# New order of the first loads, a bias row spread by TensorE, warming products first, and re-written due times in a four-layer graph kernel

## The chip, the cores and the metric

The kernel runs on one core of a Trainium2 chip. The metric is the device time of one execution in microseconds (us), taken as the median of the runs. A core has five engines that work side by side, each through its own queue and in the order of that queue: TensorE (PE in the profile; PEld is its weight load), VectorE (DVE), ScalarE (ACT), GpSimd (POOL) and SyncE (SP, which only issues DMAs). They wait for each other through semaphores.

## The reference, cut to what matters

`x` has 128 matrices of 128 x 512 in float32, `adj` is 128 x 128, the weights are 512 x 512. Four layers follow each other, each with a residual and a layer norm over the last axis:

```python
# layer 0
y = einsum('nm,bmd->bnd', adj, x)
x = layernorm(x + y @ weight + bias)
# layer 1: attention without softmax; rel is masked with adj.T and divided by its row norm
rel = adj.T * ((x @ Wq.T) @ (x @ Wk.T).T); rel = rel / norm(rel, axis=2)
x = layernorm(x + rel @ (x @ Wv.T))
# layer 2: graph attention, masked with adj
h = x @ W;  e = leaky_relu(h@a1 [:, None] + h@a2 [None, :]) * adj
x = layernorm(x + elu(softmax(e) @ h + beta * h))
# layer 3: pre[b, o, d, n] = A[b, o, n] + C[b, o, d] - A[b, o, d], A = adj @ x, C = A + b
x = layernorm(x + max(relu(pre), axis=-1))
```

## The kernel before, in words

The 128 matrices are taken in 32 groups (NG) of four (G). A group's rows lie on the 128 partitions. Each large product by a 512 x 512 matrix is a Strassen-Winograd product: seven products of half-size blocks instead of eight, with sums of blocks ahead of them. `left_factors` (line 360) makes the sums of the left side on GpSimd (s1, s2, s3, s4; its four due times stand for s1, s2, s3, s4 in that order of the list), `weight_blocks` (line 157) those of the weights on VectorE, once for the whole kernel. `product` (line 535) makes the seven products, numbered 1 to 7, on TensorE in PSUM banks ("regions": 1, 6, 7 and 4 in bank r0; 5 and 3 in r12; 2 in a bank of tag pi). What belongs to one region is added up in place, so each `out` that reads it on VectorE or ScalarE must be done before the next product adds to it. From the second group on, products 2 and 4 are themselves Strassen products (`inner_product`, the pi rows of the profile). A group's layers are: `aggregate` (p_y), the y product by w0 (r_y), `stats` and `norm`; then `turn` or `turn_blocks` with `move` (x transposed by TensorE for groups 0 and 1, by VectorE and DMAs for the others), the m product (r_m, by Wq.T Wk, which is made once as m_qk by the qk product, r_qk), `scores` (p_rel), the v product (r_v), `attend` (p_o); then `gather` (p_z), the z product (r_z), exponential and elu; then `widen` (p_a), the maximum and the last norm.

The order of all this is written out by hand. `emit(at, f)` puts a piece of code on a list with a due time, and at the end the list is sorted by due time and run (line 1243). Pieces with equal due times keep the order in which they were put on the list. The engines are wrapped by `InOrder`, so each engine's queue has its instructions in exactly that order. Due times are only an order; 28 of their units are one group. `TABLE` (line 250) has the due times of every group, `FIRST` those of groups 0 and 1 where they differ, `LAST` those of the last three, and `STEPS` (line 445) the offsets within a product with inner products. Groups overlap: while one is in layer 3, others are in layers 2, 1 and 0.

At the start, adj, x[0], x[1], the bias (read by a DMA that repeats one row of 2 KB onto 128 partitions, 256 KB), x[2] and x[3] are loaded on SP's queue, w0 on ACT's queue (lines 93 to 125), then wq, wk, wv, w2 and small things on SP's. TensorE makes two products of the identity into banks r0 and r12 (lines 132 to 135), transposes adj, and makes eight products of the identity (`WARM`, lines 144 to 146). [...]for the y product the bias is put into the bank by a copy of ScalarE (`fill` in `product`, the row ACT r_y<-bias_sb) and the products then add to it. The fill of a region precedes its first product by `lead` in due time, for group 0 by 4.4.

All lines of the profile that say L26 are instructions made through `InOrder`; they are told apart by the names of their tiles.

Of the kernel before, what the change touches and what calls it, by code (L numbers as in the profile page):

```python
# [29 lines left out]
def kernel(  # L30
# [32 lines left out]
    nc = tc.nc  # L63
# [27 lines left out]


    adj_sb = const.tile([P, P], FP)
    nc.sync.dma_start(adj_sb, adj)
    x1, x2, x3 = {}, {}, {}

    def load(g):
        x1[g] = data.tile([P, G, D], FP, tag="x1", name=f"x1_{g}", bufs=3)
        if g == 0:
            for b in range(G):  # L100
                nc.sync.dma_start(x1[g][:, b, :], x[b])
                if b == 1:
                    nc.sync.dma_start(bias_sb, on_all(bias0, D))
        else:
            sync.dma_start(x1[g], x[g * G : (g + 1) * G].rearrange("b n d -> n b d"))

    bias_sb = const.tile([P, D], FP)
    load(0)
    w0_sb = const.tile([P, K, D], FP)
    nc.scalar.dma_start(w0_sb, w0.rearrange("(k p) f -> p k f", p=P))  # L110
    wq_sb = work.tile([P, K, D], FP, tag="tv", name="wq_sb")
    nc.sync.dma_start(wq_sb, wq.rearrange("(k p) f -> p k f", p=P))
    wk_sb = work.tile([P, K, D], FP, tag="c", name="wk_sb")
    nc.sync.dma_start(wk_sb, wk.rearrange("(k p) f -> p k f", p=P))
    wv_sb = work.tile([P, K, D], FP, tag="xB", name="wv_sb")
    nc.sync.dma_start(wv_sb, wv.rearrange("(k p) f -> p k f", p=P))

    w2_sb = const.tile([P, K, D], FP)
    nc.sync.dma_start(w2_sb, w2.rearrange("(k p) f -> p k f", p=P))
    a_sb = data.tile([P, 2, D], FP, tag="x3", name="a_sb", bufs=1)  # L120
    nc.sync.dma_start(a_sb.rearrange("p s d -> p (s d)"), on_all(a2, 2 * D))
    beta_sb = const.tile([P, 1], FP)
    nc.sync.dma_start(beta_sb, on_all(beta, 1))
    b3_sb = const.tile([P, 1], FP)
    nc.sync.dma_start(b3_sb, b3.rearrange("(p o) -> p o", o=1))
# [5 lines left out]

    for tag, n in (("r0", 1), ("r12", 1)):
        for i in range(n):
            r = psum.tile([P, 2, H], FP, tag=tag, name=f"first_{tag}_{i}", bufs=n)
            pe.matmul(r, ident, ident[:, None, :].to_broadcast([P, G, P]), start=True, stop=True)
    mhalf = const.tile([P, G], FP)
    dve.memset(mhalf, -0.5)

    adjT = const.tile([P, P], FP)
# [3 lines left out]

    warm = bank("p_warm")
    for i in range(WARM):
        pe.matmul(warm[:, :P], ident, ident, start=True, stop=True)
# [99 lines left out]
    def row(at, step, n=G):  # L246
# [4 lines left out]
        load=[-21.1232], y=[0.9608, 1.8251, 2.1487, 2.7922],  # L251
        y_sums=[4.5561, 5.0639, 6.7629, 6.9969], y_inner=[5.2833, 7.5035, 7.9599, 7.7423],
        y_w=[6.4865, 10.1067, 9.7011, 18.5098, 16.5578, 25.5346, 18.8593],
        stats0=[13.0727, 13.9676, 15.6348, 14.8804], norm0=[15.6928],
        apply0=[16.441, 16.56, 17.1055, 18.4252], turn=[16.9531, 18.9169, 15.0983, 23.7872],
        turn_blocks=[17.6387, 18.378, 19.3199, 18.8892], move=[21.2268, 20.1475, 23.7935, 24.4105],
        x_sums=[25.5484, 25.8887, 25.5714, 27.1546], x_inner=[27.0248, 27.3651, 27.6181, 27.4647],
        m=[28.2059, 29.9451, 30.7559, 39.3743, 35.0579, 32.0807, 31.5941],
        scores=[35.5574, 36.2751, 36.3095, 39.6263], masked=[40.1785], squares=[41.2658],
        turn_rel=[40.8158], move_rel=[43.2987, 45.3105, 45.5881, 44.1661], inverse=[42.7358],  # L260
        v=[41.1537, 34.8028, 35.2269, 32.9135, 36.819, 44.1908, 45.5822],
        attend=[51.1788, 52.5818, 53.9439, 54.1297], residual=[51.7575, 52.9793, 54.8472, 55.5115],
        squares1=[52.1071, 55.1681, 55.5885, 56.295], dots=[52.6394, 54.6161, 55.8601, 56.5298],
        norm1=[56.6185], scale=[58.0637], apply1=[67.3359, 67.3118, 68.311, 67.3949],
        spread=[61.4852], leaky=[62.1614], weighted=[62.3481], greatest=[63.6868], exps=[63.9389],
        divide=[64.6743], turn_att=[66.48], with_beta=[55.7842], turn_blocks_2=[65.0697],
        move_2=[65.6032], gather=[70.1205, 71.0446, 73.2368, 74.4083],
        z_sums=[74.7466, 74.9675, 75.3471, 79.5091], z_inner=[76.2873, 76.452, 76.7576, 79.7843],
        z_w=[76.5238, 78.3454, 80.9549, 82.1806, 80.3108, 74.0925, 83.986],
        exp=[84.1886, 85.0555, 95.1779, 97.9857], elu=[86.5931, 86.915, 97.0853, 99.5009],  # L270
        norm2=[100.4793], apply2=[101.1271, 102.2, 101.6434, 101.6261],
        widen=[102.9021, 104.404, 104.6097, 106.3071],
        top=[104.9696, 105.5877, 105.8825, 107.7194], norm3=[108.5946],
        apply3=[109.0064, 110.4459, 109.9895, 111.6524], store=[116.2428],
# [4 lines left out]
            y=[-0.9173, 0.2561, 2.5559, 2.6098], y_sums=[5.7842, 6.1923, 7.6412, 8.0217],  # L279
            y_w=[6.656, 6.9826, 8.5177, 10.5158, 10.5177, 12.1185, 12.1169],  # L280
            stats0=[14.8567, 15.0593, 15.0036, 15.7551], norm0=[16.1054],
            m=[26.9197, 27.6264, 27.6652, 28.2251, 29.8853, 32.0185, 32.0172],
            scores=[35.9958, 37.3155, 38.45, 39.3155], masked=[39.5575], squares=[42.4727],
            turn_rel=[41.0869], move_rel=[42.4032, 42.1994, 41.3572, 41.7949],
            v=[42.7111, 44.0451, 45.3088, 46.3784, 47.3081, 48.2976, 49.1509],
            attend=[50.3341, 51.6935, 52.7247, 53.3341],
            residual=[51.2419, 52.2419, 52.8787, 54.4537],
            squares1=[51.6342, 53.6777, 54.5661, 54.7798], norm1=[56.2059],
            apply0=[17.374, 17.6244, 18.5295, 18.0555], turn=[18.8709, 19.7935, 20.9961, 21.5866],
            dots=[55.2805, 58.6316, 60.212, 60.5925], scale=[61.2871], spread=[61.7827],  # L290
            leaky=[62.1], weighted=[62.205], greatest=[64.0362], exps=[64.0854], divide=[65.2555],
            turn_blocks_2=[65.6], move_2=[67.0921],
        ),
        1: dict(
            y=[-11.6669, -10.4156, -10.312, -9.8874], y_sums=[-3.77, -3.67, -1.551, 3.0174],
            y_w=[7.0161, 7.9774, 8.126, 9.7685, 10.9791, 11.4015, 12.7041],
            stats0=[14.0438, 14.1814, 14.7308, 15.7036], norm0=[17.4806],
            attend=[49.1976, 51.8422, 53.416, 53.4184],
            apply0=[18.4423, 19.1027, 20.4894, 18.5104], turn=[21.0277, 21.0846, 21.3846, 21.542],
            x_sums=[22.8224, 24.281, 27.507, 28.0022],  # L300
# [5 lines left out]
            exp=[0.4623, 11.611, 13.6093, 21.9374], elu=[6.6028, 13.5806, 17.1367, 22.1806],  # L306
            norm2=[23.3538], apply2=[25.0389, 27.3987, 25.9338, 25.563],
            squares3=[35.4179, 39.239, 38.0926, 41.5412],
            widen=[44.4948, 56.0663, 55.0979, 58.4343], top=[44.9981, 56.3795, 60.4284, 60.9337],
            norm3=[62.9017], apply3=[64.4412, 66.5207, 68.7228, 67.9152], store=[69],  # L310
        ),
        NG - 2: dict(
            scale=[4.3047], apply1=[4.6775, 11.0377, 10.4618, 10.2756], spread=[6.9011],
            leaky=[8.5406], weighted=[8.6149], greatest=[11.14], exps=[12.7308], divide=[14.9407],
            turn_att=[19.4796], with_beta=[20.9256], gather=[33.1448, 34.2964, 34.1197, 33.8382],
            z_sums=[37.1312, 37.1799, 37.2299, 38.9411],
            z_w=[37.2, 39.2089, 40.5339, 42.6626, 45.9385, 46.5626, 47.9032],
            exp=[51.1816, 51.9016, 53.9016, 58.1278], elu=[51.9326, 54.0745, 59.5933, 63.8365],
            norm2=[65.6683], apply2=[66.9349, 67.9136, 68.7218, 69.9541],
            widen=[72.5885, 69.738, 73.9565, 76.7205], top=[73.9072, 73.9667, 75.9682, 78.4954],  # L320
            stats3=[68.0781, 73.1502, 70.7817, 73.9103], norm3=[73.9726],
            apply3=[81.0356, 88.4294, 88.4341, 88.4354], store=[91.3384],
        ),
        NG - 1: dict(
            load_w2=[-23.6669], m=[-1.0223, 1.0487, 2.4676, 3.6749, 7.9692, 8.2221, 9.9221],
            scores=[10.4191, 11.0622, 12.0436, 13.2103], masked=[14.918], squares=[15.9336],
            turn_rel=[17.0025], inverse=[19.5602],
            v=[17.0016, 19.283, 20.9796, 22.8356, 24.6364, 26.4739, 27.9989],
            attend=[30.1034, 30.2339, 30.8373, 30.4857],
            residual=[30.4, 31.4552, 33.8743, 31.7856],  # L330
            stats1=[33.7623, 34.1537, 33.9623, 34.1488], norm1=[34.3934],
            dots=[34.3979, 35.5481, 35.1904, 40.2755], scale=[40.5527],
# [87 lines left out]
    def by_columns(p, a, b, first):  # L420

        for c in range(2):
            for k in range(2):
# [21 lines left out]
    STEPS = {  # L445
        "m": (
            {
                1: (-1.2981, -0.3541),
                6: (1.724, 2.1528),
                7: (3.0677, 3.3979),  # L450
                5: (4.5184, 5.1615),
# [822 lines left out]
```

## Time and profile before

| what | us |
|---|---|
| median of 3 runs | 2141.83 (2141.7 to 2141.99) |
| the profiled execution's own time | 2141.56 |
| its span, from the first to the last instruction | 2139.7 |
| TensorE busy | 2116.7 |
| VectorE busy | 1725.1 |
| ScalarE busy | 1293.5 |
| GpSimd busy | 954.3 |
| first aggregate product (p_y) starts | 7.38 |
| first product by a weight (r_y) starts | 11.73 |
| w0 landed | 6.54 |
| x[0], x[1], bias, x[2], x[3] landed | 6.89, 7.55, 9.10, 9.74, 10.42 |
| last product ends | 2128.2 |

Times in the profile are from the start of the span. A row of the timeline has its start, its length, the engine, the operation, its output and inputs by name with the sizes, how many instructions were merged into it (xN), and in brackets how long the engine had been idle before and for whom it waited. A product of float32 appears as two passes, so that one matmul of the kernel is two instructions in the profile. A row's length includes the time in which the last pass runs out; the next pass can start before that.

### The profile page before, as it was taken

To read this page: it belongs to the slowest core of one execution; us is meant where nothing else is said; L and a number is where in the kernel's file an instruction comes from. 1 tells how busy PE (TensorE), PEld (TensorE's weight loads), DVE (VectorE), ACT (ScalarE), POOL (GpSimd) and SP (SyncE) were. 2 spreads that over 40 slices of the span, in tenths; PEclk is the share of its full clock that TensorE was granted. 3 is DMA by queue.
4 is the path that set the end of the run, shared out by engine and by line. 5 is a ranking of instruction groups with operands and counts; after the bars stand their busy time and mean duration, and the time that the engine had idled before them with its cause. 6 is when DMAs were issued, how large, how long until landed. Compare 5 with 4: busy or idle time off the path is not lost.

```text
span 2139.7 us, 36859 instructions
## 1 busy us (share of the span) xinstructions
PE 2116.7 (99%) x12325; PEld 1836.7 (86%) x12325; DVE 1725.1 (81%) x4961; ACT 1293.5 (60%) x2950; POOL 954.3 (45%) x949
## 2 busy tenths in 40 slices
PE   9999999999999999999999999999999999999996
PEld 7888888888888888888888888888888898888883
DVE  5688887878888878878878888788888788888777
ACT  3336556666566666567665566665666665676655
POOL 4244455444455444454444554444554444544431
PEclk9999999999999999999999999999999999999998
DMA  4012232221232222323222322212322213332201
GB/s 174 25 36 54 66 75 69 57 73 51 73 76 70 55 60 60 78 72 75 55 54 66 76 69 57 73 52 72 75 70 55 60 60 77 72 74 55 54 27 59
DMA packets 362524, 139.66 MB, mean 65 GB/s; under 512 B 303200, under 2 KB 318688, under 8 KB 362336
## 3 DMA queue, kind: packets, MB, share of 16 engines
q1 hardware_dynamic: 361808, 136.27, 24.9%
q8 instruction: 98, 1.61, 0.3%
q10 hardware_dynamic: 528, 1.05, 0.2%
q14 instruction: 90, 0.74, 0.1%
HBM read 56.17 MB, written 41.48 MB: 46 GB/s over the span
## 4 chain that ended last, share of the span: by engine, by line
PE 94%; DVE 3%; SPq 1%; DMA 1%; POOL 0%; issue 0%; ACT 0%; ACTq 0%; DVEq 0%; POOLq 0%
PE r_m L26 13%; PE r_y L26 13%; PE r_v L26 12%; PE r_z L26 12%; PE p_rel L26 5%; PE p_y L26 5%; PE p_o L26 5%; PE p_z L26 5%; PE p_a L26 5%; PE pi_m L26 4%; PE pi_y L26 4%; PE pi_z L26 4%; PE pi_v L26 4%; SPq L26 1%; DVE x L26 1%; DVE st L26 1%
## 5 line engine op out<-in xcount | busy, mean ns | idle before, releaser
L26 ACT ACTIVATE x<-x,nmean,rstd 128x512 f32<-128x512 f32 x384 | 285.7, 805 | 180.9 <-DVE nmean L26 180.9
L26 ACT ACTIVATE scr<-x 128x512 f32<-128x512 f32 x360 | 226.2, 628 | 73.3 <-DVE x L26 69.0
L26 POOL TENSOR_TENSOR rstd<-ve,mhalf 128x4 f32<-128x4 f32 (+1 forms) x99 | 98.7, 997 | 294.9 <-DVE ve L26 294.8
L26 DVE SCALAR_TENSOR_TENSOR scr<-x,wa 128x512 f32<-128x512 f32 x256 | 174.8, 683 | 4.6
L26 POOL TENSOR_TENSOR rn<-n,mhalf 128x4 f32<-128x4 f32 x32 | 32.7, 1023 | 307.4 <-ACT sq L26 307.4
L26 DVE TENSOR_TENSOR x<-r_y,x 128x512 f32<-128x512 f32 x194 | 129.3, 679 | 31.7 <-PE r_y L26 27.6
L26 DVE TENSOR_TENSOR c<-pi_z,c 128x128 f32<-128x128 f32 x420 | 123.5, 306 | 26.9 <-ACT c L26 18.4
L26 DVE SCALAR_TENSOR_TENSOR x<-p_o,rn,x 128x512 f32<-128x512 f32 x128 | 95.4, 745 | 58.4 <-PE p_o L26 58.1
L26 DVE TENSOR_TENSOR tT<-pi_m,tT 128x128 f32<-128x128 f32 x420 | 121.8, 305 | 22.3 <-PE pi_m L26 16.1
L26 ACT COPY r_y<-bias_sb 128x512 f32<-128x512 f32 x64 | 38.0, 593 | 161.4 <-DVE tT L26 161.3
L26 PE MATMUL p_z<-eT,x 128*128 128x128 f32 x1024 | 135.1, 275 | 0.3 <-DVE x L26 0.3
L26 POOL TENSOR_TENSOR s_x<-xT 128x512 f32<-128x512 f32 x64 | 80.6, 1280 | 121.5 <-DMA xT<-xB 73.1
L26 PEld LDWEIGHTS p_z<-eT,x 128*128 128x128 f32 x1024 | 129.2, 192 | 5.4 <-DVE x L26 1.3
L26 PE MATMUL p_a<-x,adjT 128*128 128x512 f32 x256 | 128.8, 607 | 5.1 <-ACT x L26 4.3
L26 PE MATMUL p_y<-adjT,x 128*128 128x128 f32 x1024 | 129.9, 275 | 0.5 <-DMA x<-in_x_dram 0.5
L26 PE MATMUL p_rel<-xT,tT 128*128 128x128 f32 x1024 | 129.8, 275 | 0.0
L26 ACT COPY yT<-p_y 128x512 f32<-128x512 f32 x128 | 74.8, 584 | 88.2 <-PE p_y L26 88.2
L26 PEld LDWEIGHTS p_y<-adjT,x 128*128 128x128 f32 x1024 | 124.5, 192 | 2.4 <-issue 0.7
L26 PEld LDWEIGHTS p_rel<-xT,tT 128*128 128x128 f32 x1024 | 124.7, 192 | 1.8
L26 PE MATMUL p_o<-v,relT 128*128 128x512 f32 x256 | 125.7, 594 | 0.3 <-ACT xT L26 0.2
L26 DVE TENSOR_TENSOR x<-pi_y,x 128x128 f32<-128x128 f32 x420 | 118.9, 300 | 6.3
L26 PE MATMUL r_m<-s_x,t_m 128*128 128x256 f32 x512 | 123.7, 384 | 0.0
(244 smaller groups left out, 6067.5 us busy)
## 6 DMA issues: line engine op xcount, KB each, us to landing
out_dram<-x SPq DMA_DIRECT2D x128, 256.0 KB, 2.0
x<-in_x_dram SPq DMA_DIRECT2D x31, 1024.0 KB, 7.7
xT<-xB SPq DMA_DIRECT2D x480, 64.0 KB, 2.3
relT<-relB SPq DMA_DIRECT2D x496, 16.0 KB, 1.8
eBd<-eB SPq DMA_DIRECT2D x30, 256.0 KB, 2.0
eT<-eBd SPq DMA_DIRECT2D x120, 64.0 KB, 1.9
s<-s2d SPq DMA_DIRECT2D x29, 256.0 KB, 5.1
w_sb<-in_L_gnn_weight_dram ACTq DMA_DIRECT2D x1, 1024.0 KB, 5.8
```

Source lines behind the costliest of these rows:

```text
L26: return lambda *args, **kw: self.tc.keep_in_program_order(op(*args, **kw))
```

## The change

The loads are issued on SP's queue in this order: adj, the bias, x[0] to x[3], w0, wq, wk, wv, w2, the small ones. The bias comes as one row of 512 numbers onto one partition (`bias_row`, which shares its memory with x2). A row of ones beside it is the left factor of two products of one row, which write the bias on all 128 partitions into the banks r0 and r12; ScalarE copies r12 into `bias_sb`. These products take the place of the two products of the identity. The eight warming products go ahead of the transpose of adj. The fill's lead for group 0 becomes 0.7, as for the other groups (0.2 for group 1). The due times of all tables are new; the products' arithmetic and the number of the other instructions are as before.

```diff
     adj_sb = const.tile([P, P], FP)
-    nc.sync.dma_start(adj_sb, adj)
+    sync.dma_start(adj_sb, adj)
...
             for b in range(G):
-                nc.sync.dma_start(x1[g][:, b, :], x[b])
-                if b == 1:
-                    nc.sync.dma_start(bias_sb, on_all(bias0, D))
+                sync.dma_start(x1[g][:, b, :], x[b])
...
     bias_sb = const.tile([P, D], FP)
+    bias_row = data.tile([1, D + P], FP, tag="x2", name="bias_row")
+    sync.dma_start(bias_row[:, :D], on_one(bias0, D))
     load(0)
     w0_sb = const.tile([P, K, D], FP)
-    nc.scalar.dma_start(w0_sb, w0.rearrange("(k p) f -> p k f", p=P))
+    sync.dma_start(w0_sb, w0.rearrange("(k p) f -> p k f", p=P))
...
-    for tag, n in (("r0", 1), ("r12", 1)):
-        for i in range(n):
-            r = psum.tile([P, 2, H], FP, tag=tag, name=f"first_{tag}_{i}", bufs=n)
-            pe.matmul(r, ident, ident[:, None, :].to_broadcast([P, G, P]), start=True, stop=True)
     mhalf = const.tile([P, G], FP)
     dve.memset(mhalf, -0.5)
 
+
+    warm = bank("p_warm")
+    for i in range(WARM):
+        pe.matmul(warm[:, :P], ident, ident, start=True, stop=True)
     adjT = const.tile([P, P], FP)
     pt = bank("p_adjT")
     pe.transpose(pt[:, :P], adj_sb, ident)
     dve.tensor_copy(adjT, pt[:, :P])
-
-    warm = bank("p_warm")
-    for i in range(WARM):
-        pe.matmul(warm[:, :P], ident, ident, start=True, stop=True)
...
     FIRST = {
         0: dict(
-            y=[-0.9173, 0.2561, 2.5559, 2.6098], y_sums=[5.7842, 6.1923, 7.6412, 8.0217],
-            y_w=[6.656, 6.9826, 8.5177, 10.5158, 10.5177, 12.1185, 12.1169],
...
+            y=[-1.77, 2.4, 2.4, 2.4], y_sums=[2.52, 3.99, 5.05, 4.97],
+            y_w=[3.1, 8.75, 7.87, 10.61, 10.49, 12.11, 11.88], stats0=[13.25, 13.68, 13.75, 14.7],
...
-            apply0=[17.374, 17.6244, 18.5295, 18.0555], turn=[18.8709, 19.7935, 20.9961, 21.5866],
+            apply0=[18.13, 18.21, 18.36, 18.21], turn=[18.55, 19.1, 19, 18.61],
...
         "m": (
             {
-                1: (-1.2981, -0.3541),
-                6: (1.724, 2.1528),
-                7: (3.0677, 3.3979),
...
+                1: (-1.37, -0.35),
+                6: (0.42, 2.39),
+                7: (3.25, 4.25),
...
-            lead={0: 4.4, 1: 0.2}.get(g, 0.7),
+            lead=0.7 if g != 1 else 0.2,
...
+    ones = bias_row[:, D:]
+    dve.memset(ones, 1.0)
+
+    def write_banks():
+        for tag in ("r0", "r12"):
+            r = psum.tile([P, 2, H], FP, tag=tag, name=f"first_{tag}")
+            pe.matmul(r.rearrange("p c h -> p (c h)"), ones, bias_row[:, :D], start=True, stop=True)
+        act.copy(bias_sb, r.rearrange("p c h -> p (c h)"))
+
+    emit(0.98, write_banks)
+    weight_blocks([-3.3, 3.46, 8.37, 8.61], "0", w0_sb, inner_at=[30.55, 29.43])
+    weight_blocks([12.11, 15.42, 19.01, 12.3], "k", wk_sb, tag="x2")
     qk = {"qT": wq_sb}
-    left_factors([12.1205, 12.9174, 12.3442, 13.4402], qk, "qT", "s_x", "q", 1)
-    product([14.2187, 15.0704, 15.8714, 17.2045, 18.012, 19.0486, 19.9151], "qk", by_rows, qk, "k", rows_of(lambda: m_qk), True)
-    weight_blocks([20.1618, 20.2109, 26.0084, 27.0694], "m", m_qk, inner_at=[32.2418, 27.8924])
-    each([21.5594, 22.3429, 22.1232, 22.7447], prepare_v)
+    left_factors([6.61, 8.14, 15.38, 11.96], qk, "qT", "s_x", "q", 1)
+    product([14.79, 14.84, 16.62, 16.34, 17.58, 18.97, 21.13], "qk", by_rows, qk, "k", rows_of(lambda: m_qk), True)
+    weight_blocks([19.73, 20.04, 23.34, 21.87], "m", m_qk, inner_at=[38.79, 25.15])
+    each([26.79, 25.17, 25.11, 27.44], prepare_v)
```

The seven due times of a product are those of products 1, 2, 6, 5, 7, 3 and 4, in this order. In due order the first product of the kernel (y of group 0) was 1, 2, 6, 5, 7, 4, 3 and is 1, 6, 2, 7, 5, 4, 3; the aggregates of group 0 were due one after the other with the fill of bank r0 between the second and the third, and are due now as the first, the two products of ones, the other three, and then the fill.

## Prediction

> **What bounds the kernel now.** I read the busy table and a table of stretches first, to see whether an engine is full and where it is not, then the waits of TensorE, then the timeline of the places that the change moves. The page's first part says that TensorE (PE) is the bound; in the stretches each engine's name is followed by its busy us and (x) its instructions:
>
> ```profile
> PE 2116.7 (99%) x12325; PEld 1836.7 (86%) x12325; DVE 1725.1 (81%) x4961; ACT 1293.5 (60%) x2950; POOL 954.3 (45%) x949
> ...
> 0.00:12.00 12.00, 10.10 (x55) 7.74 (x56) 3.37 (x7) 3.60 (x6) 0.70 (x6) 1.00 0.79 280
> 12.00:26.00 14.00, 13.22 (x61) 11.08 (x60) 8.73 (x11) 1.01 (x2) 10.71 (x8) 1.00 1.05 384
> 210.00:2040.00 1830.00, 1829.79 (x10807) 1600.84 (x10806) 1493.75 (x4371) 1151.53 (x2649) 850.74 (x846) 1.00 0.27 66
> 2095.00:2140.00 45.00, 28.09 (x69) 12.10 (x67) 35.30 (x104) 22.71 (x39) 7.83 (x11) 0.84 0.18 70
> ```
>
> From 210 to 2040 us PE lacks 0.21 us of 1830: a new order there can gain nothing and can only lose. What can be gained lies before 210 (the fill) and after 2040 (the drain, where VectorE (DVE) is busy 35.3 of the last 45 us and ends the chain). PE's waits before 210, in us, times, longest:
>
> ```profile
> PE r_m L26 <- DVE tT L26: 0.9, 1, 0.9
> PE r_v L26 <- DVE x L26: 0.8, 1, 0.8
> PE r_y L26 <- DVE x L26: 0.8, 1, 0.8
> PE p_y L26 <- DMA x<-in_x_dram: 0.5, 1, 0.5
> PE p_xT L26 <- ACT xT L26: 0.3, 1, 0.3
> PE p_wv L26 <- ACT xT L26: 0.2, 1, 0.2
> ```
>
> Three of them are a bank of products waiting for VectorE to read it, about 1.05 us each once the slower pass after a wait is counted. The first stretch in order of time:
>
> ```profile
> 1.36 3.78 PE L26 MATMUL first_r<-ident 128*128 128x512 f32 x4 [1.36 <-POOL ident masks.py:199]
> 4.93 0.42 PE L26 MATMUL p_adjT<-ident,adj_sb 128*128 128x128 f32 x1
> 5.15 2.40 PE L26 MATMUL p_warm<-ident 128*128 128x128 f32 x16
> 5.39 0.29 DVE L26 COPY adjT<-p_adjT 128x128 f32<-128x128 f32 x1 [4.52 <-PE p_adjT L26]
> 7.38 1.95 PE L26 MATMUL p_y<-adjT,x 128*128 128x128 f32 x16
> 9.88 2.02 PE L26 MATMUL p_y<-adjT,x 128*128 128x128 f32 x16 [0.54 <-DMA x<-in_x_dram]
> 11.73 3.62 PE L26 MATMUL r_y<-w_sb,yT 128*128 128x256 f32 x16
> 11.94 0.59 ACT L26 COPY yT<-p_y 128x512 f32<-128x512 f32 x1 [0.31 <-PE p_y L26]
> 13.72 0.69 DVE L26 TENSOR_TENSOR x<-r_y,x 128x512 f32<-128x512 f32 x1 [4.08 <-ACT r_y L26]
> ```
>
> The first weight product starts at 11.73. Before it stand 3.57 us of first_r, the warming passes, and the wait for x[2]. A pass of 512 columns takes 0.853 here ((4.93 - 1.36)/4, with 0.16 for the first) and 0.43 later (p_a x4 in 1.73); one of 128 takes 0.213, then 0.112 (p_y x16 in 1.79); eight of 256, one product of blocks, 1.73. The change of rate is at 6.0 us. Stalls are given below as what the starts of successive passes in the timeline lie apart over these pitches; the pass after a stall takes 0.1 more. New orders are the due times of the diff, sorted.
>
> [...] half rate to 6.0 us, 4.6 after the first product, and again after the idle 3.67 us at 2112.8 in the drain; idle times of 1.0 us did not halve it. [...] w0 on ACT's queue landed at 6.54 and x[0], issued beside it on SP's, not before 6.89. [...] t<-wk_sb took 1.53 us beside GpSimd, the like t<-w_sb 0.69 alone.
>
> **The loads.** w0's one DMA moves from ACT's queue, where it cost 0.46 us of issue before anything else was due, to SP's, behind x; the 256 KB of broadcast bias become 2 KB. x[0] is issued 0.4 us later, at about 1.6, but shares with nothing. SP's queue alone moved 384 GB/s in the second stretch, so from the first bytes at about 2.2 us x (1.1 MB with adj) is all in by about 5.2 and w0 (1 MB more) by 8; wq, wk, wv, w2 follow about 2.5 us sooner than now. A 2 KB DMA landed in 1.4 us (s2d<-d), adj_sb in 2.4, so the bias row is there by 3.7 and needed at 6.9. Gain in itself: the 0.54 us of p_y, and x stops holding the front.
>
> **The front on PE, new order.** Warming: 16 passes at 0.213 plus 0.16 = 3.57, 1.36 to 4.93, just what first_r took; adjT as now, copied at 5.68. PE idles 0.65. y[0] from 5.8: two slow passes, six quick ones, 1.1, to 6.9. Two bias products of two passes: 4 x 0.43 = 1.72, to 8.6 (upper end, at the half clock: 3.41; [...]). y[1] to y[3]: 3 x 0.893, to 11.3. So the front is about 0.4 us shorter than 11.73. But the fill copy of the bank of product 1 (ACT r_y<-bias_sb) is now due after the last three y, not between y[1] and y[2]; ACT takes its queue in order, so it stands behind y[3]'s copy: 11.3 + 0.2 to see the end, 0.48 to the next start (11.94 and 12.42 now), 0.60 of copy, 0.05: product 1 at 12.65, **0.9 later** than now. The ACT copy of the bias out of PSUM (0.59), the memset of ones (mhalf's took 0.06) and the difference of halves (0.42) lie beside PE.
>
> **The first product, order 1, 6, 2, 7, 5, 4, 3 in place of 1, 2, 6, 5, 7, 4, 3.** Product 6 adds into the bank that VectorE must have read after 1: 0.2 + 0.69 + 0.05, and 0.1 for the pass after a wait, 1.05 us with nothing between; its sum s2 on GpSimd is ready at 14.8, before. In return 5 stands between 7 and 4, which covers the present 1.05 (20.34 to 21.50), and the 0.19 around 15.27 go too. Seven products are 12.1; 12.65 + 12.1 + 1.05 = 25.8, against 25.06: **0.75 late**. w0's factors on VectorE lie in that time; the one that waits for w0 until 8 has only product 1's read behind it, due at 14.5.
>
> **The rest of the fill.** qk: 0.2 for its bank, 0 to 0.5, since two of wk's factors (0.69 to 1.53 each) stand ahead of that bank's last read on VectorE. Transposes and prepare_v: today three stalls of 1.0 together at 42.4 to 44.8, because prepare_v and turn fight for two banks; in the new order turn 0 and 3 stand before, 2 and 1 after qk's product 3, and m's product 1 comes between the prepare_v: gone. Layer 1's m: today 4 waits 1.1 at 53.7 for the read after 7; now 2 stands between: gone, with 0.3 kept back since VectorE reaches that read only 0.4 us ahead. y_1: ends with 4, 3 in place of 3, 4, so v's product 1 finds its bank read: 1.05 at 73.9 gone. turn 1, 2, 3 in a row before attend cost about what the two pairs cost (0.8): 0. What comes next as limit is PE itself. Sum: 0.75 + 0.2 - 1.0 - 1.1 + 0.3 - 1.05 = **-1.9 us**.
>
> **Steady groups and drain.** The sorted due times give SP's transfers in the old sequence in every group, move_rel included, and PE's with a few neighbours exchanged. I followed each: 0. The nearest to harm is product 6 of m, now ahead of the y instead of behind two of them. In the drain the sequence of stores is unchanged, and VectorE's work too; 0, between -1 and +1 (the four PE waits at 2071 to 2075 are 0.9 together).
>
> **Sum.** The profiled execution took 2141.56 us, span 2139.7 and 1.86 around it; the median of the runs is 0.27 above. 2141.56 - 1.9 + 0.27 = **2139.9**. About 0.2% (4.3 us) is what a measurement of this kernel can tell from no change.
>
> **Rivals.** (a) As worked out, 60%: 2139.9, own range 2137.8 to 2142.0, from the bounds of qk's bank, VectorE's read in m, and the drain. (b) The idle 0.65 us before y[0] [...] +1.7: 2141.6, 16%. [...] (c) The two front waits (1.35 behind the fill copy, 1.05 behind VectorE) don't appear, since ACT or VectorE see a product's end sooner, and the drain loses its 0.9: -1.9 - 2.4 - 0.9, 2136.6, 13%. Against: 0.2 us from last pass to reader is found throughout. (d) **Slower**: one wait in 29 groups. Product 6 of m adds to the bank that ACT copies after 1; these lines are of a steady group:
>
> ```profile
> 676.09 1.89 PE L26 MATMUL r_m<-xT,m_qk 128*128 128x256 f32 x8
> 678.01 0.59 ACT L26 COPY tT<-r_m 128x512 f32<-128x512 f32 x1 [1.21 <-PE r_m L26]
> 678.93 1.95 PE L26 MATMUL p_y<-adjT,x 128*128 128x128 f32 x16
> ```
>
> The copy ends at 678.60; product 6 now comes at 680.71 and would come at 678.93. It is late once ACT starts the copy over 0.3 us later; with one square still queued ahead (0.63 + 0.19), 0.5 x 29 = 14.5: 2154.4, 11%. Against: ACT was idle 1.21 us before it, and the apply that stood there moves behind. That x isn't early at all would leave 2140.4, inside (a).
>
> **Numbers.** Faster by over 0.2% is (c), 0.13; slower is (d), 0.11; within is the rest, 0.76. The range leaves out (d) and about half of (c): 2136.8 to 2143.0, the upper end from (b) with the bias products at the half clock.
>
> **What would show it.** Product 1 of r_y at 12.65 with ACT r_y<-bias_sb last before it; a wait of r_y for DVE x of about 1 us at 14.4; no such wait at v's start; p_xT and p_wv without waits; p_y at 5.8 without a wait for DMA; r_m of m at about 57.6 done instead of 58.45; PE from 210 to 2040 still within 0.3 us of full. Wrong would be: half-rate passes after 7 us, or any PE wait that comes 29 times.

## The result, and the profile after

| | kernel before | changed kernel |
|---|---|---|
| median of 16 runs each, us | 2141.81 (2141.45 to 2142.54) | 2146.1 (2141.19 to 2148.0) |
| ratio, 95% interval | | 1.0019 (1.0011 to 1.0027) |
| profiled execution, its span | 2141.56, 2139.7 | 2146.40, 2144.6 |
| first product by a weight (r_y) starts | 11.73 | 14.48 |
| first product of qk (r_qk) starts | 25.06 | 27.84 |
| first attention product (p_o) of group 4 starts | 340.77 | 342.28 |
| attention products of the last group start | 2069.71 | 2073.73 |

The changed kernel is 4.3 us slower, above the forecast range, and its runs scatter by 7 us where those of before scatter by one. The marks in the table cut the 4.9 us between the two spans into four: +2.78 up to r_qk (the forecast said +0.75), -1.27 from there to group 4 (-2.65), +2.52 in the steady groups (0), and +0.87 from the last group's attention products to the end (0, between -1 and +1).

The table of stretches of the changed kernel, with the columns as above (after each engine its busy us and instructions, then the granted clock of TensorE, the DMA share, GB/s):

```profile
0.00:12.00 12.00, 10.26 (x44) 8.49 (x45) 1.87 (x5) 3.04 (x4) 0.70 (x6) 0.87 0.80 279
...
210.00:2040.00 1830.00, 1826.75 (x10795) 1595.05 (x10794) 1505.38 (x4363) 1153.86 (x2647) 840.41 (x843) 1.00 0.27 66
2095.00:2140.00 45.00, 30.85 (x95) 15.10 (x93) 38.98 (x114) 24.65 (x45) 8.20 (x11) 0.87 0.12 47
```

TensorE is busy a little longer in the first 12 us than before (10.26 against 10.10) but gets less done in them, since the granted clock is 0.87 where it was 1.00. (The column does not count the half rate at the start: it reads 1.00 for the first 12 us of the kernel before too, whose passes ran at 0.213 us up to 6.0 us.) In the steady stretch it now lacks 3.25 us of 1830, where it lacked 0.21. Three of TensorE's waits of the changed kernel before 210 us (in us, times, longest):

```profile
PE r_y L26 <- ACT r_y L26: 1.2, 1, 1.2
PE r_y L26 <- DVE x L26: 0.9, 1, 0.9
PE p_xT L26 <- ACT x L26: 0.6, 1, 0.6
```

The two waits of r_y are those that the forecast named, the fill copy and VectorE's read after product 1. The waits of r_m, r_v and p_wv, and the wait for x[2], are gone as forecast; p_xT kept two, of 0.6 us (shown) and 0.2. The start in order of time:

```profile
5.74 1.16 PE L26 MATMUL p_y<-adjT,x 128*128 128x128 f32 x8 [0.38 <-DVE adjT L26]
...
6.83 1.98 PE L26 MATMUL first_r<-bias_row 1*128 1x512 f32 x4
...
8.74 4.58 PE L26 MATMUL p_y<-adjT,x 128*128 128x128 f32 x24
...
13.83 0.60 ACT L26 COPY r_y<-bias_sb 128x512 f32<-128x512 f32 x1
...
14.48 0.70 PE L26 MATMUL r_y<-w_sb,yT 128*128 128x256 f32 x2 [1.17 <-ACT r_y L26]
```

Up to 8.74 this is the forecast within 0.15 us: warming to 4.93, y[0] from 5.74, the two bias products of one row from 6.83 (their size reads 1x512) in 1.91. Then the 24 passes of y[1] to y[3] take 4.41 us up to the end of their last pass's turn, where 2.68 was forecast. They start 0.213 us apart until 12.2 us: the clock is at half rate from 8.76 to 12.18 us, for 3.41 us, with TensorE never idle in that time. In the chain of the front this is 1.7 of the 2.78 us.

The loss in the steady groups has one line in the waits from 210 to 2040 us:

```profile
PE pi_m L26 <- DVE tT L26: 3.2, 5, 0.7
```

Five groups of some 28 stall, by 0.79 to 0.91 us each and 0.1 more for the slow pass after it, and the others don't. One of the five, and for comparison the same place of a group that doesn't stall, both from the timeline of the changed kernel:

```profile
491.74 1.27 POOL L26 TENSOR_TENSOR s_y<-yT 128x512 f32<-128x512 f32 x1 [2.44 <-ACT yT L26]
491.76 1.80 DVE L26 SCALAR_TENSOR_TENSOR x<-m,x 128x512 f32<-128x512 f32 x1
...
493.49 0.61 DVE L26 TENSOR_TENSOR tT<-pi_m,tT 128x128 f32<-128x128 f32 x2
...
494.15 0.49 PE L26 MATMUL pi_m<-si_x,u_m 128*128 128x128 f32 x2 [0.63 <-DVE tT L26]
...
623.02 0.69 DVE L26 SCALAR_TENSOR_TENSOR x<-m,x 128x512 f32<-128x512 f32 x1
...
623.29 1.56 POOL L26 TENSOR_TENSOR s_y<-yT 128x512 f32<-128x512 f32 x1 [2.73 <-ACT yT L26]
```

VectorE's second step of elu reads two SBUF tiles (m and x). When GpSimd's first sum of the next y began 0.02 us ahead of it, it took 1.80 us; when it began 0.27 us ahead of GpSimd, 0.69, and GpSimd's sum took 1.56 instead of 1.27. VectorE's read of the inner product, the row tT<-pi_m, is queued right behind it, and TensorE waits for that read. In the kernel before the same elu is held even more often (11 of 104 between 300 and 2000 us, against 5 of 104) and TensorE never waits for it. One of the 11, with the read already done:

```profile
489.96 0.61 DVE L26 TENSOR_TENSOR tT<-pi_m,tT 128x128 f32<-128x128 f32 x2
...
491.28 1.58 DVE L26 SCALAR_TENSOR_TENSOR x<-m,x 128x512 f32<-128x512 f32 x1
```

So the holding is not new; what stands behind it is.

### The profile page after: what moved, and what is told of

It is laid out like the page before. It is cut to its first block, busy times and chain, and to the rows that moved or that the text cites. A ratio compares the mean times of both kernels' runs of the same rounds, so it can differ in the third digit from the quotient of the medians.

```text
span 2144.6 us, 36920 instructions
## 1 busy us (share of the span) xinstructions
PE 2117.0 (99%) x12325; PEld 1834.8 (86%) x12325; DVE 1738.6 (81%) x4962; ACT 1299.0 (61%) x2951; POOL 947.9 (44%) x949
## 4 chain that ended last, share of the span: by engine, by line
PE 95%; DVE 3%; ACT 1%; SPq 0%; issue 0%; POOL 0%; DMA 0%; ACTq 0%; DVEq 0%; POOLq 0%
PE r_y L26 13%; PE r_v L26 13%; PE r_m L26 13%; PE r_z L26 12%; PE p_rel L26 5%; PE p_z L26 5%; PE p_o L26 5%; PE p_a L26 5%; PE p_y L26 5%; PE pi_y L26 4%; PE pi_v L26 4%; PE pi_m L26 4%; PE pi_z L26 4%; DVE x L26 2%; PE r_qk L26 0%; SPq L26 0%
## 5 line engine op out<-in xcount | busy, mean ns | idle before, releaser
L26 PE MATMUL p_o<-v,relT 128*128 128x512 f32 x256 | 131.4, 597 | 0.1
L26 DVE TENSOR_TENSOR v<-pi_v,v 128x128 f32<-128x128 f32 x420 | 121.2, 300 | 6.2
L26 PEld LDWEIGHTS r_z<-w_sb,s_z 128*128 128x128 f32 x496 | 94.1, 190 | 37.0 <-issue 25.9
```

The source lines that it names most:

```text
L26: return lambda *args, **kw: self.tc.keep_in_program_order(op(*args, **kw))
```

## The experiments

The mends and trials are edits of the changed kernel, where nothing else is said. The kernel before was timed beside each; its medians are 2141.65 to 2141.91 us.

Theory at this point, one for each loss. Front: the half rate from 8.76 us follows from the two products of one row that stand before it, 1.91 us of them (theory R); the rival is (b) of the prediction, the idle time before y[0] (theory I). Why the hardware should do either is not shown by a trace; the runs below tell only which of the two brings the half rate. Steady groups: the held elu with a read queued behind it; the rival is the new order of TensorE's own products. Drain: its new due times.

**Full rows.** The row of the bias lies in a zeroed tile of 128 rows, and its load moves behind that of x[0]:

```diff
-    bias_row = data.tile([1, D + P], FP, tag="x2", name="bias_row")
-    sync.dma_start(bias_row[:, :D], on_one(bias0, D))
+    bias_row = data.tile([P, D + P], FP, tag="x2", name="bias_row")
+    dve.memset(bias_row[:, :D], 0.0)
...
                 sync.dma_start(x1[g][:, b, :], x[b])
+                if b == 0:
+                    sync.dma_start(bias_row[0:1, :D], on_one(bias0, D))
```

> The changed kernel, but the row of the bias lies in row 0 of a tile of 128 rows that are otherwise zero, so that the two bias products stream 128 rows in place of one: same columns, same passes, same place, same result. Theory R [...]: the passes of y[1] to y[3] run at 0.112 us in place of 0.213 from 8.7 us on, y[3] ends near 11.4, product 1 of r_y starts near 12.7 in place of 14.48, the mean clock of 0 to 12 us is 1.00 in place of 0.87; 1.8 us faster than the changed kernel. Theory I (the idle time before y[0] did it): no change, half rate from 8.7 to 12.1 us.

Measured: median 2144.42 (21 runs), ratio to the kernel before 1.0012 (1.0005 to 1.0018), 1.7 us faster than the changed kernel. Its clock in the first 12 us is 1.00, and its start reads:

```profile
6.62 1.88 PE L26 MATMUL first_r<-bias_row 128*128 128x512 f32 x4
8.34 2.89 PE L26 MATMUL p_y<-adjT,x 128*128 128x128 f32 x24
```

The 24 passes take 2.89 instead of 4.58 us, although 127 of the 128 rows carry zeros. r_qk starts at 25.84, 0.78 after the kernel before, where the prediction's working said 0.75. Theory R holds: with 128 rows in place of one, at the same place, the half rate is gone.

**Idle time filled.** Two more warming products behind the transposition of adj, so that TensorE is busy without a break from 1.36 us:

```diff
     dve.tensor_copy(adjT, pt[:, :P])
+    for i in range(2):
+        pe.matmul(warm[:, :P], ident, ident, start=True, stop=True)
```

> The changed kernel with two more warming products behind the transposition of adj, so that TensorE does not idle before y[0]. Theory I (idle time of 0.65 us): the half rate after 8.7 us goes, y[3] ends near 11.8 (y[0] starts up to 0.5 later), 1.3 to 1.8 us faster than the changed kernel. Theory R (the one-row products): the half rate comes back after the one-row products as before, y[3] ends near 13.2 to 13.6; 0 to 0.5 us slower than the changed kernel.

Measured: median 2146.5 (8 runs), ratio 1.0024 (1.0014 to 1.0034); the clock is 0.94 and 0.93 in the first two stretches.

```profile
9.47 4.48 PE L26 MATMUL p_y<-adjT,x 128*128 128x128 f32 x24
```

The passes go to half rate at 10.6 us, with no idle time of TensorE behind them (busy 10.64 of the first 12 us, all from 1.36 on). Theory I falls, and with it the cause that rival (b) gave; its size, +1.7, was that of the effect: 3.41 us at half rate cost half of that by estimate, 1.7.

**How many rows.** The same tile with 32 and with 8 rows instead of 128, one run each (`bias_row = data.tile([32, D + P], ...)` and `[8, D + P]`). For 32 rows two outcomes were open, the half rate back or the full rate kept; so they were for 8.

> The changed kernel with the bias products over 32 rows (row 0 the bias, the others zero). [...] the half rate comes back after 8.7 to 11 us for 3.4 us; [...] the passes of y[1] to y[3] stay at 0.112 us.

> The changed kernel with the bias products over 8 rows (one holds the bias, seven are zero). 32 rows kept the full rate, one row lost it. [...] y[1] to y[3] run at 0.112 us a pass; [...] half rate for 3.4 us from 8.7 to 11 us would set the bound between 8 and 32.

Measured, 32 rows first, then 8:

```profile
7.45 1.98 PE L26 MATMUL first_r<-bias_row 32*128 32x512 f32 x4
9.36 2.99 PE L26 MATMUL p_y<-adjT,x 128*128 128x128 f32 x24
```

```profile
6.68 2.18 PE L26 MATMUL first_r<-bias_row 8*128 8x512 f32 x4
8.78 4.35 PE L26 MATMUL p_y<-adjT,x 128*128 128x128 f32 x24
```

With 32 rows the full rate stays (24 passes in 2.99 us), with 8 it goes (4.35), so the bound lies between, as far as one profile each can say. As the run with 8 rows has the memset and the moved load too, these are not what brought the full rate back. The split is clean over all profiles: half rate in the seven with one-row products, the changed kernel's among them, and in the one with 8 rows; none in the one with 32 and the four with 128. In each of the eight the clock is full for 3.41 us from its first change to the full rate and then half for 3.41 us. In the full stretch the products of few rows stood for 1.6 to 1.9 us, and products of full height for at most 1.5.

**The front alone.** The kernel before with the new loads, warming and one-row bias products, and its own due times for everything else (`emit(-0.3, write_banks)` puts the bias products between y[0] and y[1]).

> The kernel before with the new front alone: loads on one queue, warming first, the row of the bias and its two one-row products between y[0] and y[1]; every due time else is that of the kernel before. Theory R (the one-row products cost a window at half rate): y[1] to y[3] at 0.213 us a pass, product 1 of r_y at 13.2 to 13.9 in place of 11.73, nothing else moves: 1.4 to 2.1 us slower than the kernel before, 2143.2 to 2143.9. If the order of the fill did the harm: product 1 of r_y at 11.4, 2141.4 to 2141.6.

Measured: median 2143.33 (13 runs), ratio 1.0008 (1.0000 to 1.0017); product 1 of r_y at 13.14, no wait in the steady groups (1728.73 us between the two attention marks, 1728.93 in the kernel before). The new front alone costs 1.7 us by the medians. In its profile product 1 comes 1.41 us later, behind passes of y[1] to y[3] at half rate again. The new order of the fill can't explain that, since this kernel has the old one.

**The read put forward.** In the steps of m, block 2:

```diff
-                2: ((-0.7, 1.51), (2.29, 3.44), (4.46, 4.94)),
+                2: ((-0.7, 1.51), (2.29, 2.5), (4.46, 4.94)),
```

> The changed kernel with one number of the steps of m changed: VectorE's read after products 6 and 3 of the inner product for block 2 is due at 2.5 in place of 3.44, which puts it ahead of the second elu of the group before instead of behind it. Theory L (VectorE's elu that reads two SBUF tiles now and then starts after a GpSimd sum and stands until that ends, 1.6 to 1.8 us in place of 0.69, and the read stood behind it): the five stalls of 0.8 to 0.9 us of pi_m behind DVE tT are gone, the steady stretch 210 to 2040 us has less than 0.3 us of idle TensorE, elu's of 1.6 us still occur; span about 4.5 us less than the changed kernel's profiled 2144.6 (about 2140.2), median near 2141.9, runs within 1 us of each other. Theory P (TensorE's own order, the block 4 products ahead of the block 2 ones, did it): stalls at pi_m stay in number and size.

Measured: median 2167.72 (4 runs), ratio 1.0119 (1.0103 to 1.0134). The expectation, near 2141.9, missed by 26 us: 28 groups now stall.

```profile
PE pi_m L26 <- DVE tT L26: 18.7, 28, 2.2
```

The timeline of this kernel shows whom they wait for:

```profile
497.13 1.57 DVE L26 SCALAR_TENSOR_TENSOR x<-m,x 128x512 f32<-128x512 f32 x1
...
498.80 0.63 ACT L26 ACTIVATE scr<-x 128x512 f32<-128x512 f32 x1 [1.80 <-DVE x L26]
...
499.43 1.05 ACT L26 COPY tT<-r_m 128x512 f32<-128x512 f32 x2
...
500.51 0.81 DVE L26 TENSOR_TENSOR tT<-pi_m,tT 128x128 f32<-128x128 f32 x3 [1.03 <-ACT tT L26]
...
501.38 0.49 PE L26 MATMUL pi_m<-si_x,u_m 128*128 128x128 f32 x2 [0.96 <-DVE tT L26]
```

The read ahead of the elu makes the elu 0.5 us later, so that GpSimd's sum now starts first almost always (here at 496.46): 25 elu's are held between 300 and 2000 us instead of 5. And a second queue is bound to the elu: ScalarE's square of its result (scr<-x) waits 1.80 us for it, ScalarE's copy of product 7 (tT<-r_m) is queued behind that square, VectorE's next read adds to what the copy writes, and TensorE waits for the read. In the table of before the copy was due between the first and the second square (3.40); in the new one it is behind the second (4.25).

**Read and copy put forward.**

```diff
-                7: (3.25, 4.25),
+                7: (3.25, 3.28),
```

> The changed kernel with two numbers of the steps of m changed: the read after products 6 and 3 of block 2's inner product due at 2.5 (was 3.44) and ScalarE's copy after product 7 due at 3.28 (was 4.25), so that each stands ahead of the second elu and of its square, as in the kernel before. Theory C (two orders made every long elu costly: VectorE's read behind the elu, and ScalarE's copy behind the square that waits for that elu; with the read alone put forward the copy became the wait of nearly all groups): no wait at pi_m behind DVE tT, whatever the number of elu's of over 1.5 us; steady stretch (from the attention products of group 4 to those of the last) 1726 to 1727 us in place of 1731.45, runs within 1 us, median 2141.5 to 2142.3. Theory P (TensorE's own new order does it): the stalls of 0.7 to 1.1 us stay.

Measured: median 2143.2 (13 runs), ratio 1.0007 (0.9998 to 1.0015), 0.9 us above what was expected. In the steady part no wait was expected: 26 elu's are held between 300 and 2000 us, and one group stalls in place of 28 (1.15 us, at 1276). Without that stall the two attention marks lie 1727.0 us apart. The rest lies in the front, where in this profile the first full rate, and with it the half rate after it, comes later than in the changed kernel's (product 1 of r_y at 15.02, not 14.48), and in the drain (71.21 us from the last attention products to the end, 70.02 in the kernel before). Theory C holds and P falls, as TensorE's order is the new one.

The one remaining stall comes in three of the four kernels with both numbers. In each of the three it is in the only group where VectorE's first step of elu, which also reads two SBUF tiles (c and x), is held as well (1.57, 1.71 and 1.75 us). In the fourth kernel no first step is held. So two held instructions in a row seem to be more than even this order can bear; no run was made to test that.

**The copy alone.**

> The changed kernel with ScalarE's copy after product 7 of m due at 3.28 (was 4.25), VectorE's read left at 3.44, behind the elu. By theory C both orders cost when an elu is held: the read alone left behind it still stalls TensorE by about 0.8 us at pi_m in each group with a held elu, some 2 to 6 groups of 28, and in no other. If the copy was the only cause: no stall.

Measured in one run: three waits at pi_m behind VectorE's read, of 2.1 us together, in the three groups with a held elu; in the others none. Each order is a cause of its own. The pairing holds in all seven profiles that have the read behind the elu: from 210 to 2040 us they have 28 held elu's and 28 stalls, each stall ending 2.2 to 2.4 us after the start of a held elu.

**The drain of before**, all of `LAST`:

> The changed kernel with the due times of the last three groups of the kernel before. Theory O (the new order of the drain costs): the wait of p_a for ACT's x at 2118 falls from 6.3 to about 3.5 us, the drain from the end of the last attention products to the last store is 0.85 us shorter, the time 0.9 less than the changed kernel's with equal stalls before. Theory S (the drain only came in a different phase): the wait stays, time the same within 0.3 us.

Measured: median 2144.7 (21 runs), ratio 1.0013 (1.0007 to 1.002). From the last group's attention products to the end it takes 70.10 us, against 70.89 of the changed kernel and 70.02 of the kernel before: Theory O. In the waits at the end, the kernel before first, then the changed kernel, then this one:

```profile
PE p_a L26 <- ACT x L26: 4.3, 2, 3.5
```

```profile
PE p_a L26 <- ACT x L26: 6.5, 2, 6.3
```

```profile
PE p_a L26 <- ACT x L26: 4.7, 2, 3.9
```

The wait for ScalarE fell as Theory O said, but two waits for VectorE (p_a behind DVE mx, 1.7 together) came beside it, so these waits alone don't show where the time went. That the due times of `LAST` cost it is shown by the length of the end: 70.89 to 71.98 us in the eight profiles with the new ones, 69.71 to 70.10 in the six with the old ones, 1.4 us apart on average, which is also what the median fell by. Which of the due times does it was not taken apart.

**The three mends together.**

> The changed kernel with the three mends together: bias products over 128 rows, the two numbers of m, the due times of the drain of the kernel before. If the three losses add up: front 1.8 less, steady stretch 1726 to 1727 us, end from the last attention products 70.1: span 2137.0 to 2137.6, median 2139 to 2139.6, below the kernel before by 2.3 to 2.9 us and near the forecast 2139.9. If they don't add (one takes the place of another): 2141 or more.

Measured: median 2140.33 (13 runs, 2139.35 to 2141.47), ratio to the kernel before 0.9993 (0.9985 to 1.0002). All 13 runs lie below the lowest of the 33 runs of the kernel before beside them (2141.52), but the interval just reaches 1. The profiled one has span 2137.8, steady part 1726.81, end 70.09; TensorE is never idle from 210 to 2040 us:

```profile
210.00:2040.00 1830.00, 1830.00 (x10817) 1598.44 (x10817) 1537.38 (x4374) 1155.30 (x2651) 852.07 (x846) 1.00 0.27 66
```

The mends add up: 1.7 (rows) + 1.4 (drain) + 2.9 (the two numbers of m) = 6.0 from their single medians, 5.8 together. A gain over the kernel before, as forecast, is not shown by this interval; that the three losses are gone is.

**The two waits of the front.** First both are taken away at once (lead 2.0 and y_0's products in the order 1, 2, 6, 5, 7, 3, 4), then the fill copy alone (lead 2.0), both on top of the three mends:

> The three mends, and the two waits of the front taken away: the copy that fills the bank of r_y ahead of the copies of y[1] to y[3] (its lead 2.0 in place of 0.7), and the products of y_0 in the order 1, 2, 6, 5, 7, 3, 4, so that no product adds into a bank that VectorE has yet to read after the last one. If the two waits are what they looked like (1.3 and 1.1 us): product 1 of r_y near 11.2 to 11.4 us, r_qk near 23.4 to 23.9, 2.2 to 2.4 us faster than the three mends alone, median 2136.7 to 2137.3. If the weights or GpSimd's sums come too late for it: less than 1 us of that.

> The three mends (bias products over 128 rows, the two numbers of m, the drain of the kernel before), and of the front's two waits only the fill copy: its lead is 2.0 in place of 0.7, so that ScalarE fills the bank of r_y ahead of the copies of y[1] to y[3]. The order of y_0's products stays. From the run with another order of y_0 as well, product 1 of r_y can start with the end of y[3] (11.4 to 12.1, by when the clock is released), 0.9 to 1.3 us sooner than with the three mends alone, and w0's factors come in time since the order is the old one: median 2139.0 to 2139.5, which beats the kernel before by 2.3 to 2.8 us. If product 6 waits longer instead (for w0's factor or GpSimd's sum): no gain over the 2140.33 of the three mends.

Measured: medians 2140.78 and 2140.35, ratios 0.9996 (0.9988 to 1.0004) and 0.9993 (0.9984 to 1.0001): no gain over the three mends. In both, product 1 of r_y starts right behind y[3] (12.05 and 12.12), and the time is given back at once. In the first, product 5 waits 1.73 us for w0's factor, queued on VectorE behind the read after product 6, and qk's first product 0.8 us for the read after product 4, which the new order left bare. In the second, product 6 waits for GpSimd's sum:

```profile
15.64 2.00 PE L26 MATMUL r_y<-t,s_y 128*128 128x256 f32 x8 [1.63 <-POOL s_y L26]
```

GpSimd begins its chain of two sums, 1.26 us each, only when y[3] is copied (at 12.98), so behind the two waits lies a third.

## Why the prediction was wrong

**The step of the front that failed** is "y[1] to y[3]: 3 x 0.893, to 11.3". In the sum it was given no other value, although the sentence before it bounded the bias products themselves by the half clock; only rival (b) had one, for another cause. The bias products ran at full rate; the passes after them did not: 4.41 us in place of 2.68. This is also the sign that the prediction had named as wrong, half-rate passes after 7 us. The warming, the adjT copy, the 1.72 of the bias products (1.91 measured), the late fill copy and VectorE's read after product 1 came as worked out. x was in time; w0 landed at 9.8 us instead of by 8, at no cost here. With 128 rows the whole front came out at +0.78 against +0.75. That this is so close is in part luck: product 1 came 0.26 us sooner than worked out and the seven products took 0.3 longer, and in the three mends, where the full rate first came later (y[0]'s eight passes took 1.55 us, 1.16 with the full rows alone), the front is +1.20. The half rate lasted 3.41 us in the changed kernel, and in the run with the idle time filled it came with no idle time ahead of it. The trace of before has no product of one row, and the prediction worked out only how long such a product takes; that part holds, since the passes of one row and of 128 are both 0.43 us apart.

**The step of the steady groups that failed** is "I followed each: 0". The orders of TensorE and of the DMA queue were compared; that VectorE's read went from ahead of the second elu to behind it, and ScalarE's copy from ahead of the second square to behind it, was not priced, since VectorE had room by its busy time. The room was there with the elu at 0.69 us, not at 1.6 to 1.8. The mark "still within 0.3 us of full" was the right one to look at, and failed with 3.25. The same 0 was wrong on the other side too, as was "a new order there can gain nothing": without stalls a group takes 64.88 us where it took 64.95, about 2 us over the steady part, which the stalls ate (2.5 + 2 is about the 4.6 of the five stalls). Busy by the profile, TensorE still lost 0.29 us in a group of the kernel before to passes that started late, and 0.24 in one of the changed kernel.

**The fill** came back by 1.27 instead of 2.65 us: r_m's and v's waits went as said (1.1 and 1.05), but the three stalls of the transposes, 1.0 together, were replaced by one of 0.84 at 41.3 us (the wait p_xT behind ACT x), not by none; the other half microsecond is spread over stalls of less than 0.3 and was not taken apart. **The drain** cost 0.87 in this profile, within the bound of 1 that was given, but 1.4 on the average of the profiles and 1.8 to 2.0 in three of eight. An unchanged sequence of stores was not enough for a 0; through which wait the new due times cost it stays open.

**The rivals.** (b) had the size of the front's loss and the wrong cause, (c) named waits that were there, and (d) was the right kind, a wait in the products of m that comes back group by group, at the wrong place: product 6 never waited in the steady groups, the inner product did, and in some groups only. The scatter has at least three sources: in the profiles the first full rate of the clock comes between 4.9 and 7.4 us (the kernel before may absorb part of that in its wait for x[2], which was not tried), the number of stalling groups changes from run to run (3 to 6 in the profiles with the order of the changed kernel), and so does the length of the new drain (by 1.1 us).

## What to carry to other kernels

Products of one or eight rows kept TensorE busy by the profile here (1.91 and 2.10 us) and were still followed or overlapped by 3.41 us at half rate, so in this kernel the row is better spread with a zero-padded tile of 128 rows (the 24 passes after it in 2.89 us, not 4.58), at no cost in time (VectorE's memsets, 0.50 us in the first 5, lie beside the loads). A read that TensorE waits for was badly placed behind a VectorE instruction that read two SBUF tiles and could start under a GpSimd sum, and behind a ScalarE instruction that waited for such a one (1.80 us): take that instruction at its held length (1.6 to 1.8 us here, not 0.69) when an order is judged. When one queue's order was followed through a new table, the others' neighbours have to be followed too, and a wait taken away early in a chain is worth only the distance to the next one.

## What the hardware showed unexpectedly

- Bias products over 1 and over 8 rows were followed by 3.41 us at half rate, those over 32 and 128 rows were not, with the same columns, passes and place (1.91, 2.10, 1.91 and 1.72 us from their first pass to the next product, for 1, 8, 32 and 128 rows; with 8 rows the half rate began within the last pass).
- Real idle time did the same once among the steady groups. In the kernel with the read put forward TensorE waited 2.22 us up to 1290.34, and the clock was at half rate from 1290.68 to 1294.09; in the 3.41 us before that TensorE was busy for 1.19. Waits of 1.73 and 1.63 us in the front (the two runs of the front's waits) were not followed by half rate: the granted clock of both is 1.00 from 12 to 26 us.
- The held elu follows who starts first. Between 300 and 2000 us, GpSimd's first sum of y was running at the elu's start in 11 of 11 held ones of the kernel before, 5 of 5 of the changed kernel and 26 of 26 of the three mends, and in none of those that took 0.69. 0.02 us made the difference between 0.69 and 1.80: at 491.76 us of the changed kernel the sum had begun 0.02 us ahead, the elu took 1.80 and the sum 1.27; at 947.69 both began within 0.01 us, the elu took 0.69 and the sum 1.82. The 16 held elu's of the first two kernels all ended 0.55 us after that sum. VectorE's read tT<-r_m,tT, with one input in a bank, took 0.69 in all 54 cases of the changed kernel although a GpSimd instruction was running at the start of each. Why it is so, the traces do not show.
